# State-space layer with a routed inner layer on one core: matmul order inside a bank, a margin in the planner, and the share of GpSimd

## The chip, the core and the metric

The kernel runs on one core of a Trainium2 chip. The core has five engines that run at the same time, each through its own instructions in order: TensorE (PE, matmul, with the weight load shown apart as PEld), VectorE (DVE), ScalarE (ACT), GpSimd (POOL) and SyncE (SP, which here starts all transfers). They wait for each other on semaphores. The metric is the device time of one execution in microseconds; lower is better. All data is f32.

## What is computed

The input is `u` of 4 sequences, 2048 steps and 256 features. A layer normalization, a selective state-space layer and a residual come first; then a second normalization, a top-2 routed inner layer with low-rank expert parts, and a residual.

```python
def _ssm_forward(u, W_in, b_in, W_x, b_x, W_dt, b_dt, A_log, D, W_out, b_out):
    u_inner = u @ W_in.T + b_in
    x, z = jnp.split(u_inner, 2, axis=-1)
    dbc = x @ W_x.T + b_x
    ...
    delta = jax.nn.softplus(delta_raw @ W_dt.T + b_dt)
    A = -jnp.exp(A_log)
    def step(h, xs):
        dt_t, x_t, Bt, Ct = xs
        dA = jnp.exp(dt_t[..., None] * A)
        dB = dt_t[..., None] * Bt[:, None, :]
        h = h * dA + x_t[..., None] * dB
        y_t = jnp.einsum('bdn,bn->bd', h, Ct)
        return (h, y_t)
    ...
    y = y + x * D
    y = y * (z * jax.nn.sigmoid(z))
    return y @ W_out.T + b_out

def _L0_ffn_ref(x, Wg, bg, Wi, Wo, A, B):
    ...
    base = jnp.einsum('bsd,fd->bsf', x, Wi)
    lora_low = jnp.einsum('bsd,erd->bser', x, A)
    lora = jnp.einsum('bser,efr->bsef', lora_low, B)
    h = jax.nn.relu(base[:, :, None, :] + lora)
    expert_out = jnp.einsum('bsef,df->bsed', h, Wo)
    return jnp.einsum('bse,bsed->bsd', w, expert_out)
```

There are 512 inner channels, 16 states for each, 4 experts of rank 4, and 1024 inner features; `w` holds the weights of the two best experts.

## The kernel before

**Tiles and states.** Time is cut into 16 chunks of 512 steps, four for each sequence. The 512 channels of a chunk are 4 blocks `d` of 128 partitions. For each block and each of the 16 states `n` there is one tile of 128 x 512: with 4 x 16 = 64 of these "states" in a chunk, the main loop (line 924) runs over 1024. Their order is two halves of two blocks each; within a half, groups of four: first block with two `n`, then second block with the same two.

**One state.** `decay` (791): ACT writes exp(a * delta) into one of three PSUM tiles, dA. `enter` (796): POOL multiplies xdt (delta times x) with B, for two states in one operation, into one of three double tiles dBx. `scan` (808): DVE runs the recurrence over dA and dBx, in place in dA. `read` (822): the product of the state with C. DVE writes it as hC, or POOL as hP; POOL does it where `shared` (817) says so, now the first state of each group of four. [...] the scan of a shared state writes to SBUF, as hS. `keep` (831): ACT copies the last column as the carry to the next chunk of the sequence. `sum_y` (836): PE turns the product by four transposing matmuls that add up in the PSUM tile y of its block. `sum_y` runs two loop steps behind the scan, three for a shared state.

**Work beside the loop.** For each chunk, lists of steps run along with the loop. `front` (392) is the normalization of the next chunk, its input projection, delta and softplus, xdt, and the gate with silu; `tail` (524) is the output projection; `ffn` (558) is the second normalization, the routing and the inner layer. Softplus and silu each make ACT load a function table before and after. `layernorm_T` (324) takes statistics on DVE (`stats`), then the reciprocal root on POOL (`rstd`: four small operations), then scales on ACT and transposes on PE.

**The inner layer.** Each chunk has eight rounds `k` (four blocks of 128 steps, two halves of the features). `p_base` starts a PSUM bank with the base product. `p_low` adds to it the low-rank part for the second-best expert, and for the round before the difference that turns this into the best one. `a_relu` takes the ReLU with the expert's weight out of the bank after each. `p_hT` adds both by transposing matmuls into another bank, `a_hT` copies it, and `p_down` makes the down products from two rounds. Three banks of the pool `ps` serve all these and the front's projections; `takes` and `gives` on a step count them.

**Who sets the order.** `Pacer` (45) writes the instructions of each engine in a fixed order at build time. It carries a planned clock for each engine, and each `Step` has a cost. After each scan and each product `fill` (106) lets in those steps whose planned start is close enough to DVE's planned clock; `ready` (126) is the rule. `force` (147) writes a step, with all it needs, at a deadline; `drain` writes what is left after the loop. Nothing of the planning is seen at run time: an engine that meets an operand that is not there waits, and all behind it on that engine.

**The names `xdts`.** Before the loop, `front(0, ...)` returns chunk 0's steps as `xdts` (897). In the loop, line 954 gives the same name the list of the next chunk. Line 952, at state 27, forces `xdts[-1]`.

Of the kernel before, what the change touches and what calls it, by code (L numbers as in the profile page):

```python
# [44 lines left out]
class Pacer:  # L45
# [80 lines left out]
    def ready(self, x):  # L126
        t = self.start(x)
        if t is None:
            return False
        v = self.now["dve"]  # L130
        if self.quiet and x.engine == "act" and x.cost > self.MOST:
            return False
        if x.engine == "dve":
            t = max([y.end for y in x.after if y.engine != "dve"], default=0.0)
            return t + self.LATENCY + self.MARGIN <= v
        return t <= v + self.BEGIN[x.engine] and (t + x.cost <= v + self.END[x.engine] or t <= v - 0.5)

    def drain(self):
# [30 lines left out]
def ssm_moe_layer_kernel(  # L169
# [35 lines left out]
    NN = 2  # L205
    NG = N // NN
    ND2 = 2
    NH = ND // ND2
    CPB = T // TC
    NCHUNK = B * CPB  # L210
    BANKS = 3

    const = ctx.enter_context(tc.tile_pool(name="const", bufs=1))
# [4 lines left out]
    small = ctx.enter_context(tc.tile_pool(name="small", bufs=2))  # L218
# [51 lines left out]
    bm_sb = const.tile([32 * TOPK, F], F32, tag="bm_sb", name="bm_sb")  # L270
# [5 lines left out]
    mhalf = const.tile([P, NJ], F32, tag="mhalf", name="mhalf")  # L276
# [47 lines left out]
    def layernorm_T(src, dst, name, then=None):  # L324

        q = {}

        def stats(j):
            if j == 0:
                q["mv"] = small.tile([P, NJ, 2], F32, tag=f"mv{name[0]}", name=f"mv_{name}")  # L330
            x = small.tile([P, 6], F32, tag="st", name=f"st_{name}_{j}")
            dve.bn_stats(x, src()[:, j, :])
            dve.bn_aggr(q["mv"][:, j, :], x)

        def rstd():

            ve = small.tile([P, NJ], F32, tag="ve", name=f"ve_{name}")
            q["rstd"] = small.tile([P, NJ], F32, tag="rstd", name=f"rstd_{name}")
            q["nmr"] = small.tile([P, NJ], F32, tag="nmr", name=f"nmr_{name}")
            pool.tensor_scalar_add(ve, q["mv"][:, :, 1], EPS)  # L340
            pool.tensor_tensor(q["rstd"], ve, mhalf, ALU.pow)
            pool.tensor_tensor(ve, q["mv"][:, :, 0], q["rstd"], ALU.mult)
            pool.tensor_scalar_mul(q["nmr"], ve, -1.0)

        def norm(j):
            q["xn", j] = work.tile([P, DM], F32, tag=f"xn{j}", name=f"xn_{name}_{j}", bufs=1)
            act.activation(
                q["xn", j], src()[:, j, :], AF.Identity,
                scale=q["rstd"][:, j : j + 1], bias=q["nmr"][:, j : j + 1],
            )  # L350

        def turn(k):
            q["pt", k] = mm_tile(f"pt_{name}_{k}")
            for j in range(NJ):
                pe.transpose(
                    q["pt", k][:, j * P : (j + 1) * P], q["xn", j][:, k * P : (k + 1) * P], ident
                )

        def out_(k):
            if k == 0:  # L360
                q["dst"] = dst()
            act.copy(q["dst"][:, k, :], q["pt", k])

        steps = [Step("dve", 0.54, lambda j=j: stats(j)) for j in range(NJ)]
        steps += [Step("pool", 1.95, rstd)]
        steps += [Step("act", 0.5, lambda j=j: norm(j), locks=j == 0) for j in range(NJ)]
        norms = steps[-1]
        turns = [
            Step("pe", 0.45, lambda k=k: turn(k), after=[norms], takes=1, unlocks=k == KM - 1)
            for k in range(KM)  # L370
        ]
        outs = [Step("act", 0.5, lambda k=k: out_(k), after=[turns[k]], gives=1) for k in range(KM)]
        if then:
            steps.append(then)
        return steps + turns + outs
# [182 lines left out]
    def ffn(c):  # L558

        s = st[c]  # L560
        q = {}
# [96 lines left out]
        HF = F // 2  # L658
        NK = 2 * NJ

        def p_base(k):
            j, half = divmod(k, 2)
            pm = q["z", k] = mm_tile(f"pz_{c}_{k}")
            for m in range(KM):
                pe.matmul(
                    pm, lhsT=s["x2T"][:, m, j * P : (j + 1) * P], rhs=wi_sb[:, m, half * HF : (half + 1) * HF],
                    start=(m == 0), stop=False, skip_group_check=True,
                )

        def p_low(k):  # L670
            for slot, x in ((1, k), (0, k - 1)):
                if 0 <= x < NK:
                    j, half = divmod(x, 2)
                    r = slice(32 * slot, 32 * slot + ER)
                    pe.matmul(
                        q["z", x], lhsT=s["lowT"][r, j * P : (j + 1) * P],
                        rhs=bm_sb[r, half * HF : (half + 1) * HF], start=False, stop=True,
                        skip_group_check=True,
                    )

        def a_relu(k, slot):
            h = q["h", k, slot] = work.tile([P, HF], F32, tag=f"h{slot}", name=f"h{slot}_{c}_{k}")
            act.activation(h, q["z", k], AF.Relu, scale=s["topv"][:, slot, k // 2 : k // 2 + 1])
# [36 lines left out]
        steps = layernorm_T(lambda: s["u"], lambda: new_x2T(c), f"f{c}")  # L720
# [14 lines left out]
        last = steps[-1]  # L735
        for x in steps[-3:]:
            x.after = [steps[steps.index(x) - 1]] + held.get("low", [])
        z1s, hs, copies = [], [], []
        bases = [Step("pe", 1.75, lambda k=k: p_base(k), after=[last], takes=1) for k in range(NK)]
        steps.append(bases[0])  # L740
        for k in range(NK + 1):

            low = Step(
                "pe", 1.06 if 0 < k < NK else 1.05, lambda k=k: p_low(k), after=bases[k : k + 1] + z1s[-1:]
            )
            steps.append(low)
            if k:
                hs.append(Step("act", 0.57, lambda k=k: a_relu(k - 1, 0), after=[low], gives=1))
                steps.append(hs[-1])
            if k < NK:  # L750
                z1s.append(Step("act", 0.57, lambda k=k: a_relu(k, 1), after=[low]))
                steps.append(z1s[-1])
            steps += bases[k + 1 : k + 2]
            if k:
                steps.append(Step("pe", 0.88, lambda k=k: p_hT(k - 1), after=[hs[-1]], takes=1))
                steps.append(Step("act", 0.5, lambda k=k: a_hT(k - 1), after=[steps[-1]], gives=1))
                copies.append(steps[-1])
            for j in range(NJ):
                if k == min(2 * j + 3, NK):
                    for h in range(2):  # L760
                        steps.append(
                            Step("pe", 1.75, lambda j=j, h=h: p_down(j, h), after=[copies[2 * j + 1]], takes=1 - h)
                        )
                    steps.append(Step("dve", 0.33, lambda j=j: add(j), after=[steps[-1]], gives=1))
# [51 lines left out]

    def shared(i):

        c, ib, d, n = states[i]
        return n % NN == 0 and d % ND2 == 0  # L820

    def read(i):
        c, ib, d, n = states[i]
# [70 lines left out]

    spare = small.tile([P, 1], F32, tag="spare", name="spare", bufs=1)
    act.activation(spare, mhalf[:, 0:1], AF.Softplus)
    f, g, dbc, xdts = front(0, front_norm(0))
    pacer.add(f)
    pacer.force(f[2 * NJ])
    join_x()  # L900
# [4 lines left out]
        load_bc(i, 0)  # L905
    for i in range(2):
        load_bc(i, 1)
    pacer.force(xdts[0])

    act.activation(a_sb, a_sb, AF.Exp)  # L910
    dve.tensor_scalar_mul(a_sb, a_sb, -1.0)
    pacer.add(g)
    for i in range(0, AHEAD_B, NN):
        pacer.force(xdts[states[i][2]])
        X[i] = X[i + 1] = pacer.run("pool", 2.32, lambda: enter(i))
    for i in range(AHEAD_A + 1):
        A[i] = pacer.run("act", 0.63, lambda: decay(i))
# [6 lines left out]
    for i in range(M + 4):  # L924
# [24 lines left out]
        if i < M:  # L949
            at = i % PER  # L950
            if i == PER // NH - AHEAD_B - 1:
                pacer.force(xdts[-1])
            if states[i][0] + 1 in deadline:
                dbc, xdts = deadline[states[i][0] + 1]
                if at == PER - 3 * NN * ND2 - 2:
                    pacer.force(dbc)
                if at == PER - AHEAD_B - 6:
                    pacer.force(xdts[0].after[0])
                if at == PER - AHEAD_B - 1:
                    pacer.force(xdts[-1])  # L960
            S[i] = pacer.run("dve", 1.2 if states[i][0] % CPB else 1.14, lambda: scan(i), [A[i], X[i]])
# [72 lines left out]
```

## Time and profile before

| | us |
|---|---|
| median of 3 runs (lowest to highest) | 2129.7 (2126.46 to 2132.01) |
| profiled execution: its own time | 2129.43 |
| its span | 2127.7 |

| group of the page | count | mean ns |
|---|---|---|
| DVE scan into dA, with carry | 576 | 1279 |
| DVE scan into hS, with carry | 192 | 1271 |
| DVE product hC | 768 | 670 |
| POOL product hP | 256 | 1276 |
| POOL product dBx | 512 | 2363 |
| ACT decay dA | 1024 | 693 |
| ACT ReLU h | 256 | 680 |

Each row of the profile names an engine, the output and inputs by the program's names, shapes, count, busy time and mean. Behind the bar stands the idle time of the engine just before these instructions and what ended it. An f32 matmul is two records: the 256 base matmuls stand as x512. Nearly all instructions pass through one helper and so carry its line, L30; they are told apart by their tiles. Idle time that belongs to an engine with time to spare costs nothing.

### The profile page before, as it was taken

How to read it: one execution, taken by the hardware profiler on the slowest of the kernel's cores; microseconds unless marked ns; L12 is line 12 of the kernel's file. 1: busy time of each engine (PE TensorE's matmuls, PEld its weight loads, DVE VectorE, ACT ScalarE, POOL GpSimd, SP SyncE). 2: the span in 40 equal slices, each digit the busy share in tenths (PEclk: the TensorE clock that was granted, in tenths of full speed). 3: DMA queues.
4: the chain of work that ended last, by engine and by line, in shares of the span. 5: the costliest groups of instructions: out<-in, count | busy, mean ns of one | idle time of the engine just before them, and what ended most of it. 6: DMA issues, size and time to landing. Idle time of an engine off the chain costs nothing.

```text
span 2127.7 us, 28591 instructions
## 1 busy us (share of the span) xinstructions
PE 1873.9 (88%) x9504; PEld 1284.0 (60%) x9504; DVE 1855.8 (87%) x2423; ACT 1441.7 (68%) x2898; POOL 1709.4 (80%) x1084
## 2 busy tenths in 40 slices
PE   7768788998889989899899988989899998989978
PEld 4445555665566665657666565766657575666655
DVE  4899898999989989999989998999989999999810
ACT  5857667667676667676767777676677867766522
POOL 5898888989878878888888888888888888878600
PEclk9859799998999999999999999999999999989989
DMA  7454344445444443434435454444535444444200
GB/s 218 144 165 152 127 150 149 149 147 161 151 139 151 149 140 138 169 130 149 163 130 164 140 167 132 147 152 139 169 130 173 136 141 149 138 149 140 98 10 10
DMA packets 106132, 300.70 MB, mean 141 GB/s; under 512 B 12864, under 2 KB 39104, under 8 KB 105984
## 3 DMA queue, kind: packets, MB, share of 16 engines
q1 hardware_dynamic: 105984, 298.88, 42.8%
q8 instruction: 74, 1.21, 0.2%
q14 instruction: 74, 0.61, 0.1%
HBM read 289.41 MB, written 9.44 MB: 140 GB/s over the span
## 4 chain that ended last, share of the span: by engine, by line
PE 25%; DVE 20%; ACT 12%; issue 5%; POOL 1%; DVEq 0%; POOLq 0%; ACTq 0%
DVE dA L30 9%; PE pz L30 9%; PE y L30 5%; PE pf L30 5%; ACT dA L30 5%; DVE hC L30 4%; DVE hS L30 4%; PE phT L30 3%; ACT L30 2%; ACT h L30 1%; PE pin L30 1%; ACT delta L30 1%; ACT g L30 1%; DVE u L30 1%; DVE plg L30 1%
## 5 line engine op out<-in xcount | busy, mean ns | idle before, releaser
L30 POOL TENSOR_TENSOR dBx<-xdt,B 128x1024 f32<-128x1024 f32 x512 | 1207.8, 2363 | 187.5 <-DVE dA L30 157.3
L30 ACT ACTIVATE dA<-delta,a_sb 128x512 f32<-128x512 f32 x1024 | 706.8, 693 | 143.0 <-DVE hC L30 66.8
L30 DVE TENSOR_TENSOR_SCAN dA<-dA,carry,dBx 128x512 f32<-128x512 f32 x576 | 726.4, 1279 | 62.6 <-ACT dA L30 51.0
L30 PE MATMUL y<-ident,hC 128*128 128x128 f32 x3072 | 490.7, 291 | 36.6 <-DVE hC L30 36.5
L30 DVE TENSOR_TENSOR hC<-dA,C 128x512 f32<-128x512 f32 x768 | 514.1, 670 | 0.2 <-issue 0.2
L30 PEld LDWEIGHTS y<-ident,hC 128*128 128x128 f32 x3072 | 386.1, 150 | 181.3 <-issue 73.6
L30 POOL TENSOR_TENSOR hP<-hS,C 128x512 f32<-128x512 f32 x256 | 326.6, 1276 | 5.1 <-issue 4.1
L30 PE MATMUL pz<-wi_sb,x2T 128*128 128x512 f32 x512 | 271.7, 657 | 25.2 <-ACT hT L30 15.4
L30 DVE TENSOR_TENSOR_SCAN dA<-dA,dBx 128x512 f32<-128x512 f32 x192 | 231.2, 1220 | 35.3 <-ACT dA L30 30.5
L30 DVE TENSOR_TENSOR_SCAN hS<-dA,carry,dBx 128x512 f32<-128x512 f32 x192 | 244.1, 1271 | 18.6 <-ACT carry L30 10.6
L30 PE MATMUL pf<-wo_sb,hT 128*128 128x256 f32 x1024 | 243.4, 383 | 11.6 <-ACT hT L30 9.4
L30 PE MATMUL pin<-xnT,w_in_sb 128*128 128x512 f32 x512 | 245.9, 612 | 5.5 <-ACT g L30 3.6
L30 ACT COPY carry<-dA 128x1 f32<-128x1 f32 x576 | 90.1, 157 | 208.5 <-DVE hC L30 206.5
L30 ACT ACTIVATE h<-pz,topv 128x512 f32<-128x512 f32 x256 | 165.4, 680 | 74.1 <-PE pz L30 73.4
L30 PEld LDWEIGHTS pf<-wo_sb,hT 128*128 128x128 f32 x1024 | 186.5, 190 | 41.6 <-ACT hT L30 14.4
L30 PEld LDWEIGHTS y<-ident,hP 128*128 128x128 f32 x1024 | 128.3, 148 | 96.3 <-issue 56.7
L30 PE MATMUL y<-ident,hP 128*128 128x128 f32 x1024 | 167.1, 288 | 18.7 <-POOL hP L30 18.7
L30 PEld LDWEIGHTS pz<-wi_sb,x2T 128*128 128x128 f32 x512 | 95.2, 207 | 124.9 <-issue 76.2
L30 PE MATMUL pz<-bm_sb,lowT 16*128 16x512 f32 x512 | 167.9, 660 | 0.0
L30 PE MATMUL phT<-ident,h 128*128 128x128 f32 x1024 | 139.7, 281 | 21.3 <-ACT h L30 16.8
L30 PEld LDWEIGHTS pin<-xnT,w_in_sb 128*128 128x128 f32 x512 | 92.3, 197 | 93.1 <-issue 75.2
L30 PEld LDWEIGHTS phT<-ident,h 128*128 128x128 f32 x1024 | 120.8, 145 | 44.2 <-ACT h L30 19.5
(94 smaller groups left out, 1784.8 us busy)
## 6 DMA issues: line engine op xcount, KB each, us to landing
B<-bc SPq DMA_DIRECT2D x256, 512.0 KB, 3.7
C<-bc SPq DMA_DIRECT2D x256, 512.0 KB, 3.7
ua<-in_u_dram SPq DMA_DIRECT2D x16, 512.0 KB, 5.5
u<-in_u_dram SPq DMA_DIRECT2D x16, 512.0 KB, 4.4
out_dram<-u SPq DMA_DIRECT2D x16, 512.0 KB, 4.8
w_in_sb<-in_w_inT_dram SPq DMA_DIRECT2D x2, 512.0 KB, 4.7
wi_sb<-in_wiT_dram SPq DMA_DIRECT2D x1, 1024.0 KB, 6.7
wo_sb<-in_woT_dram SPq DMA_DIRECT2D x1, 1024.0 KB, 10.4
```

The costliest lines, as they stand in the source:

```text
L30: return self._tc.keep_in_program_order(f(*args, **kwargs))
```

## The change

Five edits. `shared` gives POOL the products of states 0, 3, 6, 9 and 12 of every 16, five instead of four. `layernorm_T` does the negated mean and the added epsilon on DVE after the last statistics, and two small operations on POOL remain; the planned cost of that step falls from 1.95 to 1.35. In the inner layer the low-rank part of the second-best expert starts the bank, and the base product is added to it; the first ReLU follows the base product. `ready` gets a rule of its own for an ACT step that follows a PE step: it is let in only once PE's planned end lies half a microsecond back. And the first chunk's `xdts` get a name of their own.

```diff
@@ Pacer.ready
+        if x.engine == "act" and any(y.engine == "pe" and y.end + 0.5 > t for y in x.after):
+            t = max(y.end for y in x.after) + 0.5
+            return t <= v + self.BEGIN["act"] and self.now["act"] + 0.5 >= t
         return t <= v + self.BEGIN[x.engine] and (t + x.cost <= v + self.END[x.engine] or t <= v - 0.5)
@@ layernorm_T, stats and rstd
+            if j == NJ - 1:
+                q["nm"], q["ve"] = q["mv"][:, :, 0], q["mv"][:, :, 1]
+                dve.tensor_scalar_mul(q["nm"], q["nm"], -1.0)
+                dve.tensor_scalar(q["ve"], q["ve"], EPS, None, ALU.add)
...
-            pool.tensor_scalar_add(ve, q["mv"][:, :, 1], EPS)
-            pool.tensor_tensor(q["rstd"], ve, mhalf, ALU.pow)
-            pool.tensor_tensor(ve, q["mv"][:, :, 0], q["rstd"], ALU.mult)
-            pool.tensor_scalar_mul(q["nmr"], ve, -1.0)
+            pool.tensor_tensor(q["rstd"], q["ve"], mhalf, ALU.pow)
+            pool.tensor_tensor(q["nmr"], q["nm"], q["rstd"], ALU.mult)
...
-        steps += [Step("pool", 1.95, rstd)]
+        steps += [Step("pool", 1.35, rstd)]
@@ ffn, p_base and p_low
-            pm = q["z", k] = mm_tile(f"pz_{c}_{k}")
+            pm = q["z", k]
...
-                    start=(m == 0), stop=False, skip_group_check=True,
+                    start=False, stop=True, skip_group_check=True,
...
+                    if slot:
+                        q["z", x] = mm_tile(f"pz_{c}_{x}")
...
-                        rhs=bm_sb[r, half * HF : (half + 1) * HF], start=False, stop=True,
+                        rhs=bm_sb[r, half * HF : (half + 1) * HF], start=bool(slot), stop=not slot,
@@ ffn, the rounds
-        bases = [Step("pe", 1.75, lambda k=k: p_base(k), after=[last], takes=1) for k in range(NK)]
-        steps.append(bases[0])
+        bases = []
         for k in range(NK + 1):
             low = Step(
-                "pe", 1.06 if 0 < k < NK else 1.05, lambda k=k: p_low(k), after=bases[k : k + 1] + z1s[-1:]
+                "pe", 1.06 if 0 < k < NK else 1.05, lambda k=k: p_low(k), after=[last] + z1s[-1:], takes=int(k < NK)
             )
             steps.append(low)
             if k:
                 hs.append(Step("act", 0.57, lambda k=k: a_relu(k - 1, 0), after=[low], gives=1))
                 steps.append(hs[-1])
             if k < NK:
-                z1s.append(Step("act", 0.57, lambda k=k: a_relu(k, 1), after=[low]))
-                steps.append(z1s[-1])
-            steps += bases[k + 1 : k + 2]
+                bases.append(Step("pe", 1.75, lambda k=k: p_base(k), after=[low]))
+                z1s.append(Step("act", 0.57, lambda k=k: a_relu(k, 1), after=bases[-1:]))
+                steps += [bases[-1], z1s[-1]]
@@ shared
-        c, ib, d, n = states[i]
-        return n % NN == 0 and d % ND2 == 0
+        return i % 16 in SHARED
@@ before and in the loop
+    SHARED = (0, 3, 6, 9, 12)
...
-    f, g, dbc, xdts = front(0, front_norm(0))
+    f, g, dbc, first_xdts = front(0, front_norm(0))
...
-                pacer.force(xdts[-1])
+                pacer.force(first_xdts[-1])
```

More of the change, by code (lines that the diff above doesn't have):

```diff
@@ L333, in stats @@
             dve.bn_aggr(q["mv"][:, j, :], x)
+            if j == NJ - 1:
+                q["nm"], q["ve"] = q["mv"][:, :, 0], q["mv"][:, :, 1]
+                dve.tensor_scalar_mul(q["nm"], q["nm"], -1.0)
+                dve.tensor_scalar(q["ve"], q["ve"], EPS, None, ALU.add)
         def rstd():
-            ve = small.tile([P, NJ], F32, tag="ve", name=f"ve_{name}")
             q["rstd"] = small.tile([P, NJ], F32, tag="rstd", name=f"rstd_{name}")
             q["nmr"] = small.tile([P, NJ], F32, tag="nmr", name=f"nmr_{name}")
-            pool.tensor_scalar_add(ve, q["mv"][:, :, 1], EPS)
-            pool.tensor_tensor(q["rstd"], ve, mhalf, ALU.pow)
-            pool.tensor_tensor(ve, q["mv"][:, :, 0], q["rstd"], ALU.mult)
-            pool.tensor_scalar_mul(q["nmr"], ve, -1.0)
+            pool.tensor_tensor(q["rstd"], q["ve"], mhalf, ALU.pow)
+            pool.tensor_tensor(q["nmr"], q["nm"], q["rstd"], ALU.mult)
         def norm(j):
@@ L907, in ssm_moe_layer_kernel @@
         load_bc(i, 1)
-    pacer.force(xdts[0])
+    pacer.force(first_xdts[0])
     act.activation(a_sb, a_sb, AF.Exp)
@@ L913, in ssm_moe_layer_kernel @@
     for i in range(0, AHEAD_B, NN):
-        pacer.force(xdts[states[i][2]])
+        pacer.force(first_xdts[states[i][2]])
         X[i] = X[i + 1] = pacer.run("pool", 2.32, lambda: enter(i))
```

## The prediction

> **What bounds the kernel now.** I read the busy table and the slices first, then the busy time by stretch, the waits, and the timelines of one silu and of the tail.
>
> ```profile
> PE 1873.9 (88%) x9504; PEld 1284.0 (60%) x9504; DVE 1855.8 (87%) x2423; ACT 1441.7 (68%) x2898; POOL 1709.4 (80%) x1084
> ...
> DVE  4899898999989989999989998999989999999810
> ...
> POOL 5898888989878878888888888888888888878600
> ...
> L30 POOL TENSOR_TENSOR dBx<-xdt,B 128x1024 f32<-128x1024 f32 x512 | 1207.8, 2363 | 187.5 <-DVE dA L30 157.3
> ```
>
> The averages do not choose between DVE, PE and POOL. The slices show the shape: DVE is full until about 2010 us, and then two slices are almost without it. So the span is three pieces. The first scan starts at 31.6 us (timeline). The last sum over states ends on PE at 2018.4, so the loop of 1024 states takes 1986.8, or 1.94 a state. The tail, with the inner layer of the last two chunks on PE, takes 2127.7 - 2018.4 = 109.3.
>
> Busy time by half chunk (32 states each; columns: length, then busy PE, PEld, DVE, ACT, POOL, granted clock, DMA share, GB/s):
>
> ```profile
> 1455.96:1512.07 56.11, 54.31 (x310) 39.94 (x309) 54.97 (x63) 34.80 (x57) 48.19 (x26) 1.00 0.47 151
> 1512.07:1578.08 66.01, 56.82 (x267) 38.08 (x266) 59.71 (x90) 51.60 (x102) 56.37 (x41) 0.87 0.48 152
> ```
>
> The quick half has DVE at 98%, POOL at 86%. The slow half, with softmax, normalizations, softplus and silu, leaves DVE 6.3 us idle. DVE paces the loop; POOL mostly waits for DVE to free a buffer (157.3 us). What holds DVE is ACT:
>
> ```profile
> DVE dA L30 <- ACT dA L30: 81.5, 129, 6.1
> ...
> ACT dA L30 <- DVE hS L30: 65.4, 78, 1.6
> ACT hT L30 <- PE phT L30: 61.9, 62, 3.9
> ACT h L30 <- PE pz L30: 40.7, 53, 3.7
> ```
>
> (The waits between 31.6 and 2018.4: total, times, longest.) DVE also waits 21.0 us for ACT's carry copies before scans into hS. Meanwhile ACT, in order, stands 61.9 + 40.7 us at PE results of the inner layer. The decay it owes DVE stands behind them.
>
> **Products moved to GpSimd.** 256 of 1024 go to POOL now, 320 after: 64 fewer on DVE. Records on DVE overlap, so I take the spacing of starts:
>
> ```profile
> 1273.89 0.67 DVE L30 TENSOR_TENSOR g<-g,py 128x512 f32<-128x512 f32 x1
> 1274.48 0.67 DVE L30 TENSOR_TENSOR hC<-dA,C 128x512 f32<-128x512 f32 x1
> 1275.07 1.27 DVE L30 TENSOR_TENSOR_SCAN hS<-dA,carry,dBx 128x512 f32<-128x512 f32 x1
> 1276.26 0.66 DVE L30 TENSOR_TENSOR hC<-dA,C 128x512 f32<-128x512 f32 x1
> 1279.01 1.29 DVE L30 TENSOR_TENSOR_SCAN dA<-dA,carry,dBx 128x512 f32<-128x512 f32 x1 [2.09 <-ACT dA L30]
> ```
>
> A product costs 1275.07 - 1274.48 = 0.59 us: 64 x 0.59 = **-38** of pure DVE time. The scan costs the same either way (1279 ns into dA, 1271 into hS).
>
> Against that, a state without a product on DVE makes the next scan come 0.59 sooner, and then ACT's decay is late. After the hS scan at 1351.21 the scan at 1353.24 starts 0.84 after the product before it, not 0.59, its idle marked as a wait for ACT's dA: 0.25. I find it at about half to two thirds of such places between 1263 and 1334. With 0.2 for each of 64 new places: **+13** (0 if the new places have their decay in time; +38 if every one gives all back).
>
> The skill speaks against the move: GPSIMD Engine Reference, Engine selection, gives elementwise products with two inputs to VectorE, GpSimd being about twice as slow. The rows agree on the ratio (hP 1276 ns, hC 671), and by the rule alone 64 x 1.276 = 82 us come in for 38 out, +44. But those 82 count only on the path, and the 157.3 us that POOL waits for DVE can hold them. So I take the trace's sum and keep the rule's as the ground of the slower rival. The cover is thin in the quick half: 48.2 of 56.1 busy, two more products (+2.6), and the order of instructions puts the four xdt of the next chunk (4 x 1.27 = 5.1) at about state 36 of 64, from the slow into the quick half. That makes 55.9 of some 55.5: at par. POOL may start a dBx four scans and their products before it is needed, some 7 us, of which its own 2.36 is part; so POOL can run some 4.5 late, and a burst of 5.1 hardly shows. PE then waits longer for hP (18.7 us over 15 waits now), which DVE does not feel, since no hC waits for PE now. I charge nothing to the forecast.
>
> **LayerNorm.** Of four small POOL operations per normalization two go (228 and 242 ns, x32: POOL -15 us, off the path). DVE gains two on 128x4. Nearest rows: a dependent operation of that size follows the next in 0.21 (reciprocal 1285.72, product 1285.93), an independent one in 0.10 (1290.67 to 1290.77). The first waits for the statistics, so 0.2: 64 x 0.2 = **+13** (6 to 14). DVE is the pacing engine, so it is paid in full.
>
> **Low-rank part first, and the margin.** The matmuls are the same and equally long (660 ns for the low-rank, 657 for the base), so PE's work does not change. A bank is taken one base product later, and the two ReLUs come apart: now they run as a pair (1.27 us on ACT, between two decays), afterwards one has the base product and the other the transposes as cover. The margin lets an inner-layer ACT step into the order only 0.5 us after PE's planned end. DVE's waits for ACT are 81.5 + 7.8 + 21.0 plus small ones, about 111. At the start lie 12. The 32 table-loading blocks for silu and softplus (2.09 lost at the one above, 1.58 and 0.74 at others; 1.4 on average) keep about 45, as silu is forced at the same states. The places after hS hold about 27. The last 27 are what ACT's standing at PE can cause, and I take half: **-14** (0, nothing, to -45, all of it and most of the places). What is queued behind an ACT step that waits is the next decay, and behind it the scan.
>
> **First delta.** The forced step at state 27 meant the first chunk's last xdt, but the name had been rebound to the next chunk's; all of that chunk's front was forced early. It cost DVE 6.07 us, its longest wait for dA (scan at 89.99). After, softplus 1 comes at state 55, at a block like any other (about 2): **-4**, once (0 to -6).
>
> **Tail.** By the order of instructions, after the last sum 15 of chunk 14's 32 inner bank matmuls, 40 of 64 transposes and 24 of 32 down products are left now; afterwards all of them, so 17, 24 and 8 more. In the dense tail a round takes 3.84 (bank products 2.9, transposes 0.94) and a set of 8 down products 3.6: 17 x 0.72 + 24 x 0.12 + 8 x 0.45 = 19 us more. But now PE has a hole there: the output projection's matmuls end at 2053.6, the routing of chunk 15 keeps PE nearly empty until 2072.9, and the first base product then takes double:
>
> ```profile
> 2071.89 1.06 PE L30 MATMUL plT<-ident,lowm 128*64 128x128 f32 x4 [6.05 <-POOL lowm L30]
> 2072.75 3.62 PE L30 MATMUL pz<-wi_sb,x2T 128*128 128x512 f32 x4
> ...
> 2077.59 1.98 PE L30 MATMUL pz<-wi_sb,x2T 128*128 128x512 f32 x4
> ```
>
> After, the projection stands before chunk 14's rounds, and the routing lies inside them. From the last sum: 2.5 (copy, transposes, gate), 7.2 projection, 4.2 other route matmuls, two inner layers of 8 x 3.84 + 4 x 3.6 = 45.1 each, 1.5 at the end of the second, 1.5 of round waits, and 4.3 from the last matmul to the end: 111. So **+2** (-3 if the waits of 0.68 before each pair of down products go, +19 if nothing hides).
>
> **Sum.** -38 + 13 + 13 - 14 - 4 + 2 = -28, against the span of 2127.7: 2100. The profiled execution took 2129.43, 1.7 more than its span, and the median of 2129.7 lies 0.3 above that. So **2102**.
>
> **Rivals.**
> - *ACT was the real brake* (0.18): the margin removes most of what DVE waits for outside the table loads, 45 instead of 14, and new places cost nothing. 2102 - 31 - 13 = 2058; with half of the second, 2066. For it: 102 us of standing at PE. Against: half lies where DVE is not waiting.
> - *Hidden anyway* (0.15): the places after hS give back all 38, or the later steps of the inner layer keep all of chunk 14's 19 us in the tail. +25 or +17 on the forecast: 2127 or 2119, say 2123. For it: one place in two waits already, and the order does leave a whole layer behind.
> - *GpSimd becomes the bound, slower* (0.17): in the quick halves, if each of the 16 dBx keeps its wait of about 0.5 for its scan (0.53 and 0.58 in the timeline near 1350) although POOL has 55.9 to do. A half then takes up to 55.9 + 8 = 64, where the forecast has 56. If a third of these waits stays, 58.6: 16 x 2.6 = 42 on the forecast, 2144. It decides once POOL's work and waits together pass DVE's some 55.5. Against: an engine that is behind finds its scan already done.
> - That the change does not do what it says is shut out: the order has 320 products on POOL and 704 on DVE.
>
> **How the numbers follow.** Forecast 0.50 at 2102, its own range 2082 to 2118 from the unknown costs. With the rivals, 2064 to 2140 leaves out the far ends of the first and the last, under 2 in 10. A change of 0.3% is 6.4 us, about what this measurement can tell from none. Faster: all of the forecast, the ACT case, and half of the hidden one, 0.75; the same 0.07; slower 0.18.
>
> **What would show it.** hC x704 and hP x320, and DVE's busy time down by some 30. POOL's busy about +67, its wait for DVE's dA below 157.3 and few DVE waits for POOL (else the third rival). ACT's waits for PE phT and pz well below 61.9 + 40.7, and DVE's for ACT dA near 70. No 6 us wait near state 27. The last sum near 1987, and a tail of about 111 without the hole after the projection. A loop no shorter than 1986 would make the prediction wrong, as would a tail of 125.

## The result and the profile after

| | before, us | after, us |
|---|---|---|
| median of 4 runs (lowest to highest) | 2130.64 (2126.46 to 2132.01) | 2097.06 (2088.33 to 2101.31) |
| span of the profiled execution | 2127.7 | 2086.4 |
| first scan to last sum, 1024 states | 1986.8 | 1943.3 |
| the same, DVE busy / DVE idle | 1841.2 / 145.6 | 1834.6 / 108.7 |
| from the last sum to the end | 109.3 | 111.2 |

The ratio is 0.9841 [0.9825, 0.9857]: 33.6 us less. The profiled execution of after is the quickest of its four, 8.7 below their median, so a difference of spans shows some 9 us more than one of medians. The predicted 2102 lies 5 us above the result.

These are the busy table, two rows of the slices, and three of the costliest groups, all from the page of after:

```profile
PE 1844.4 (88%) x9504; PEld 1275.2 (61%) x9504; DVE 1851.3 (89%) x2423; ACT 1429.9 (69%) x2898; POOL 1764.6 (85%) x1084
...
DVE  4989999998989999999999999999999999999810
POOL 5999999898989989898888998889899898989700
...
L30 POOL TENSOR_TENSOR dBx<-xdt,B 128x1024 f32<-128x1024 f32 x512 | 1206.2, 2361 | 106.4 <-DVE dA L30 40.7
...
L30 DVE TENSOR_TENSOR hC<-dA,C 128x512 f32<-128x512 f32 x704 | 471.8, 670 | 0.0
L30 POOL TENSOR_TENSOR hP<-hS,C 128x512 f32<-128x512 f32 x320 | 407.5, 1273 | 7.9 <-DVE hS L30 3.9
```

The 64 products have moved (704 and 320), POOL is 55 us busier, and it waits 40.7 us for DVE's dA where it waited 157.3. DVE, which lost 64 products, is only 4.5 us less busy over the whole span. That is the first thing that does not fit.

The waits between the first scan and the last sum of after (total, times, longest):

```profile
DVE dA L30 <- ACT dA L30: 58.9, 79, 3.0
...
ACT dA L30 <- DVE hS L30: 48.1, 65, 3.0
...
ACT h L30 <- PE pz L30: 25.4, 39, 3.4
...
ACT hT L30 <- PE phT L30: 9.0, 19, 1.0
```

ACT now stands 34.4 us at the inner layer's results, where it stood 102.6, and DVE waits 58.9 us for its decay, not 81.5. So the table says where the 43.5 us of the loop come from: 36.9 are idle time of DVE, and only 6.6 are its work. Not all of that idle time is the margin's doing, as u_ln shows below.

The work has gone into two groups that the prediction put at 13 us. They stand in the groups of after, kept apart by shape (busy, mean ns):

```profile
L30 DVE TENSOR_SCALAR mv_a<-mv_a 128x4 f32<-128x4 f32 x32 | 26.2, 863 | 0.6
...
L30 DVE TENSOR_SCALAR mv_f<-mv_f 128x4 f32<-128x4 f32 x32 | 12.1, 424 | 0.6
```

Together 38.3 us, as much as the 64 products were worth. On mv_a an operation on 128 x 4 takes 863 ns on average, longer than a product on 128 x 512 (670). The answer for the tile mv_a (lowest, median, highest ns; first and last start) puts it beside a neighbour of the same size on the same tile:

```profile
L30 DVE BATCH_NORM_AGGREGATE mv_a<-st_a x64: 181/182/184, 5.1 to 1689.3; 128x2 f32<-128x6 f32 x64
L30 DVE TENSOR_SCALAR mv_a<-mv_a x32: 155/544/2398, 7.0 to 1689.7; 128x4 f32<-128x4 f32 x32
```

The aggregate is always alike; the new operations take anything from 155 to 2398 ns. Two stretches of the timelines of DVE and POOL in after show what decides (start, length in us; x2 joins two operations):

```profile
1069.28 2.69 DVE L30 TENSOR_SCALAR mv_a<-mv_a 128x4 f32<-128x4 f32 x2
1069.59 2.35 POOL L30 TENSOR_TENSOR dBx<-xdt,B 128x1024 f32<-128x1024 f32 x1
...
171.09 0.24 DVE L30 TENSOR_SCALAR mv_f<-mv_f 128x4 f32<-128x4 f32 x2
171.41 1.01 POOL L30 TENSOR_TENSOR rstd_f<-mv_f,mhalf 128x4 f32<-128x4 f32 x1 [1.23 <-DVE mv_f L30]
```

In the first, the pair on DVE ends at 1069.28 + 2.69 = 1071.97, and POOL's dBx at 1071.94. In the second POOL stands idle, waiting for this very pair, and the pair takes 0.24. All records of after say the same. Of its 64 small operations 26 last more than 260 ns, and each of these ends 23 to 30 ns after an operation of POOL; in none of the other 38 does an operation of POOL run from before its start until after its end. So the reading to be tested is that these small operations are *held* on DVE until POOL's operation has ended. The longest, 2636 ns on mv_f, outlasts the end of a product on POOL and the whole dBx that follows it. The Trainium skill has a rule for it, which the prediction did not weigh: SBUF — State Buffer, Who interferes with whom. By it VectorE has a second pair of ports that it shares with GpSimd under an exclusive lock; `tensor_scalar` may enter a mode that takes that pair, and the loser blocks fully; an operation with two SBUF inputs contends with GpSimd's reads, while one with at most one SBUF input, outside those modes, does not. The product hC, which reads dA from PSUM and C from SBUF, agrees: each of its 704 records lies between 656 and 686 ns, with POOL 85% busy. So does the routing's comparison, a `tensor_scalar` that reads the PSUM tile plg:

```profile
L30 DVE TENSOR_SCALAR m<-plg 128x16 f32<-128x16 f32 x32 | 4.1, 169 | 0.6
```

Its 32 records lie between 164 and 174 ns, though 12 of them fall wholly within an operation of POOL.

### The profile page after: what moved, and what is told of

The parts are those of the page before. It is cut to its first block, busy times and chain, and to the rows that moved or that the text cites. A ratio compares the mean times of both kernels' runs of the same rounds, so it can differ in the third digit from the quotient of the medians.

```text
span 2086.4 us, 28685 instructions
## 1 busy us (share of the span) xinstructions
PE 1844.4 (88%) x9504; PEld 1275.2 (61%) x9504; DVE 1851.3 (89%) x2423; ACT 1429.9 (69%) x2898; POOL 1764.6 (85%) x1084
## 5 line engine op out<-in xcount | busy, mean ns | idle before, releaser
L30 POOL TENSOR_TENSOR dBx<-xdt,B 128x1024 f32<-128x1024 f32 x512 | 1206.2, 2361 | 106.4 <-DVE dA L30 40.7
L30 DVE TENSOR_TENSOR_SCAN dA<-dA,carry,dBx 128x512 f32<-128x512 f32 x528 | 662.4, 1278 | 49.1 <-ACT dA L30 41.4
L30 PE MATMUL y<-ident,hC 128*128 128x128 f32 x2816 | 442.7, 290 | 34.8 <-DVE hC L30 34.6
L30 DVE TENSOR_TENSOR hC<-dA,C 128x512 f32<-128x512 f32 x704 | 471.8, 670 | 0.0
L30 PEld LDWEIGHTS y<-ident,hC 128*128 128x128 f32 x2816 | 352.5, 150 | 120.0 <-DVE hC L30 52.3
L30 POOL TENSOR_TENSOR hP<-hS,C 128x512 f32<-128x512 f32 x320 | 407.5, 1273 | 7.9 <-DVE hS L30 3.9
L30 DVE TENSOR_TENSOR_SCAN hS<-dA,carry,dBx 128x512 f32<-128x512 f32 x240 | 305.2, 1272 | 15.6 <-ACT dA L30 8.3
L30 PE MATMUL pz<-wi_sb,x2T 128*128 128x512 f32 x512 | 257.6, 627 | 0.0
L30 PEld LDWEIGHTS y<-ident,hP 128*128 128x128 f32 x1280 | 162.7, 149 | 147.4 <-issue 79.7
L30 PE MATMUL y<-ident,hP 128*128 128x128 f32 x1280 | 209.8, 289 | 39.8 <-POOL hP L30 39.7
L30 DVE TENSOR_TENSOR_SCAN dA<-dA,dBx 128x512 f32<-128x512 f32 x176 | 211.1, 1219 | 26.1 <-ACT dA L30 17.5
L30 PEld LDWEIGHTS pin<-xnT,w_in_sb 128*128 128x128 f32 x512 | 91.9, 196 | 90.4 <-issue 75.0
```

The costliest lines, as they stand in the source:

```text
L30: return self._tc.keep_in_program_order(f(*args, **kwargs))
```

## Experiments on LayerNorm

**u_ln: after, with the four small operations on POOL again.** The theory: the held operations cost the changed kernel their length. The rival: DVE has slack for them.

```diff
-                dve.tensor_scalar_mul(q["nm"], q["nm"], -1.0)
-                dve.tensor_scalar(q["ve"], q["ve"], EPS, None, ALU.add)
...
+            pool.tensor_scalar_add(ve, q["mv"][:, :, 1], EPS)
             pool.tensor_tensor(q["rstd"], ve, mhalf, ALU.pow)
...
+            pool.tensor_scalar_mul(q["nmr"], ve, -1.0)
```

> The changed kernel with the two small LayerNorm operations back on GpSimd, as before (four operations there, none added on VectorE); the other four edits kept. Port theory: in the changed kernel's trace the 64 VectorE operations on 128x4 show 38.3 us of records instead of the 13 predicted, and the long ones end within 0.1 us of a GpSimd operation, so they are held while GpSimd has the shared port. Then taking them away gives VectorE some 36 us back, part of it lost again to waits for ScalarE: 2065 to 2082, ratio to before 0.970 to 0.978, and no stretched small operation on VectorE. Rival, cover: these stalls lie where VectorE would wait for a decay anyway, and GpSimd gets 15 us more to do: no gain, 2092 to 2102, ratio 0.982 to 0.987.

Measured: 2072.18 us (2069.74 to 2072.95), ratio to before 0.9728 [0.9712, 0.9744]. This is 25 us quicker than after, and the quickest of all kernels here. The busy table of its page:

```profile
PE 1839.2 (89%) x9504; PEld 1268.8 (61%) x9504; DVE 1815.6 (88%) x2359; ACT 1430.3 (69%) x2898; POOL 1779.1 (86%) x1148
```

POOL does 64 operations and 14.5 us more, and the kernel is still quicker; DVE has 35.7 less. In the loop alone DVE's busy time falls by 35.3 against after and its idle time grows by 18.6 (127.3 against 108.7), which leaves 16.7. So about half of what the operations hold DVE is given back: while it stands, ACT's decays get ahead. DVE's wait for ACT's dA, 58.9 in after, is 70.6 here. The cost is 17 us by the two profiled loops and 25 by the medians (24 when each is set against before on its own chip). That DVE was held is shown by its records. How much of the net cost is the hold is not: the edit also puts the planned cost of the step on POOL back to 1.95, and in the two traces the order of instructions on PE, ACT and DVE differs from the first chunks on. A kernel with the order of after and unheld operations was not run.

**o_ln: before, with this edit alone.** The kernel before, where POOL is 80% busy and not 85%, gets the lines that u_ln loses.

```diff
+                dve.tensor_scalar_mul(q["nm"], q["nm"], -1.0)
+                dve.tensor_scalar(q["ve"], q["ve"], EPS, None, ALU.add)
...
-            pool.tensor_scalar_add(ve, q["mv"][:, :, 1], EPS)
...
-            pool.tensor_scalar_mul(q["nmr"], ve, -1.0)
```

> The kernel before with the LayerNorm edit alone; TensorE's order of instructions is that of before. Port theory: 64 small operations on VectorE are held by GpSimd, 20 to 38 us of records instead of 13 (GpSimd is less busy here, 80% instead of 85%, so nearer the lower end), and GpSimd's 15 us less buys nothing: 2142 to 2160, ratio 1.006 to 1.014. Rival, by the prediction's price of 0.2 us each and cover by waits: 2126 to 2142, ratio 0.998 to 1.006.

The order on PE did not stay that of before: the traces differ from the first chunk on, where the transposes of the normalization stand at other places. The planned cost of the step, 1.35 instead of 1.95, is part of this edit.

Measured: 2136.82, ratio 1.0029 [1.0017, 1.0041]. It is slower, but by 6 us, inside the range of the rival and below that of the theory. The records are shorter here, 17.6 + 6.7 = 24.3 us, with means of 593 and 253 ns. DVE's busy time in the loop grew by 22.9, its idle time fell by 21.3 (145.6 to 124.3). So it is held here too, and in the loop, 1.5 us longer in all, gets nearly all of it back: DVE has more waits here to get it back from. The tail of this profiled execution is 5.5 longer (114.8), and that is not LayerNorm's: PE has the same 378 matmuls there and is busy 95.7 us with them, where it was busy 90.4 before, at a granted clock of 0.86 and not 0.91. So of the 6 us by the medians LayerNorm may have as little as 1.5. The price of a held operation is not a constant: it is what DVE does not have to wait for anyway.

**lnTT: after, with two-input operations in place of the tensor_scalar pair.** The narrow theory: only `tensor_scalar` takes the shared pair, so another operation is not held. The wide one: any operation of DVE with a second SBUF input is.

```diff
-                dve.tensor_scalar_mul(q["nm"], q["nm"], -1.0)
-                dve.tensor_scalar(q["ve"], q["ve"], EPS, None, ALU.add)
+                dve.tensor_tensor(q["nm"], q["nm"], mone, ALU.mult)
+                dve.tensor_tensor(q["ve"], q["ve"], meps, ALU.add)
...
```

> The changed kernel with the two small VectorE operations of each LayerNorm as tensor_tensor against constant tiles of -1 and epsilon, so with two inputs in SBUF[...]. If only the two-port mode is held (port theory in its narrow form), the 64 operations take 0.16 to 0.25 us each, 10 to 16 us in all: 2074 to 2086. If any second read through the shared port is held while GpSimd reads[...], records stay stretched, 25 us or more in all, and the time stays at the changed kernel's: 2088 to 2102.

Measured: 2096.47, ratio 0.984 [0.9823, 0.9858], the time of after, with the same order of instructions on PE, ACT and DVE. Two of its groups:

```profile
L30 DVE TENSOR_TENSOR mv_a<-mv_a,meps 128x4 f32<-128x4 f32 x16 | 18.1, 1132 | 0.0
...
L30 DVE TENSOR_TENSOR mv_a<-mv_a,mone 128x4 f32<-128x4 f32 x16 | 11.0, 685 | 0.6
```

With the pair on mv_f (10.9 and 2.5) this makes 42.5 us. The wide theory holds: both forms are held, and again each record over 260 ns ends with an operation of POOL, 17 to 24 ns after it. That the page's mode of `tensor_scalar` is what held the first form is not shown, as a trace does not name the mode. In its favour: in after, the reciprocal on 128 x 4, also in place in SBUF with one input, takes 177 or 178 ns in all 16 records, 8 of them wholly within an operation of POOL.

## Experiments on the products and the first delta

**u_shared: after, with four products of 16 on POOL.**

```diff
-    SHARED = (0, 3, 6, 9, 12)
+    SHARED = (0, 4, 8, 12)
```

> The changed kernel with four of 16 products on GpSimd, as before; the other four edits kept. By the prediction's sum (38 us less on VectorE, 13 given back after hS scans) it is 25 us slower than the changed kernel: 2117 to 2127. Rival, given back: GpSimd's load and the earlier scans eat it all: within 5 us of the changed kernel, 2092 to 2102.

Measured: 2119.46, ratio 0.9947 [0.9929, 0.9965], 22 us above after. DVE's busy time in the loop is 1861.6, 27 more than in after, and its small operations are held for 25.2 us, not 38.3: a less busy POOL holds them less, which hides 13 of the 38. The two profiled executions lie 31 apart, 24 in the loop and 8 in the tail (119.2), where PE again waits 6.04 us for the routing of the last chunk. In the loop the products are worth those 24 here and 34 without the LayerNorm edit (o_first to o_sharedfirst, below). That the longer held operations are the reason for this difference is likely, but not shown.

**o_shared: before, with five of 16 alone.**

```diff
-        c, ib, d, n = states[i]
-        return n % NN == 0 and d % ND2 == 0
+        return i % 16 in SHARED
```

> The kernel before with only the five of 16 products. By the prediction's sum -38 + 13 = -25, as taking it out of the changed kernel cost 22: 2103 to 2111. Rival: without the margin the earlier scans wait more for ScalarE and half is lost: 2112 to 2122, VectorE's waits for dA above 95 us.

Measured: 2106.52, ratio 0.9886 [0.9865, 0.9907], 24.8 less. The number fits and hides something. From the timeline of its DVE, near state 27:

```profile
83.73 0.67 DVE L30 TENSOR_TENSOR hC<-dA,C 128x512 f32<-128x512 f32 x1
108.66 1.23 DVE L30 TENSOR_TENSOR_SCAN dA<-dA,dBx 128x512 f32<-128x512 f32 x1 [24.26 <-ACT dA L30]
```

DVE stands still for 24 us, once. It is the forced front of the next chunk, which cost 6.07 us at this place before. The other edits of after meet the same place, so the name `first_xdts` has to be looked at together with the products.

**u_first, o_first and o_sharedfirst: the name.** u_first is after with the old name; o_first is before with only the new one; o_sharedfirst is before with five products and the new name.

u_first:

```diff
-                pacer.force(first_xdts[-1])
+                pacer.force(xdts[-1])
...
```

> The changed kernel with the old name for the first chunk's xdt, so that the next chunk's front is forced at state 27; the other four edits kept. TensorE's order differs in the first chunks only. Prediction: 4 us slower than the changed kernel, a wait of VectorE of about 6 us for a decay near 90 us, 2096 to 2106. Rival: the forced work is only moved, and the first 64 states end at the same time: 2092 to 2100.

Measured: 2116.64, ratio 0.9932 [0.9907, 0.9956], 20 above after.

o_first:

```diff
-                pacer.force(xdts[-1])
+                pacer.force(first_xdts[-1])
...
```

> The kernel before with only the first chunk's xdt under a name of its own. In the changed kernel the old name cost a wait of 23 us, because with the margin nearly nothing of the next front had been let in by state 27. Theory: here much of that front is in by then (its first projection stands at state 15), the wait at state 27 was 6.07 us, so the edit alone brings 4 to 8 us: 2122 to 2127, and no wait of over 4 us near 90 us. Rival: the name is worth 20 us by itself: 2107 to 2114.

Measured: 2122.83, ratio 0.9963 [0.9948, 0.9977], 8.5 less than before (5 to 11 by the interval). In the profiled execution the first 64 states are 2.2 shorter and the loop 8.0. The rest comes in later chunks, where all engines have the order of before, so that it is no work that the name moved; its cause is not shown.

o_sharedfirst:

```diff
-        return n % NN == 0 and d % ND2 == 0
+        return i % 16 in SHARED
...
-                pacer.force(xdts[-1])
+                pacer.force(first_xdts[-1])
...
```

> The kernel before with the five of 16 products and the first chunk's own name, without margin, new bank order and LayerNorm edit. With the five products alone VectorE stood 24.3 us at the forced front of state 27, so the products, not the margin, keep the next front from being in by then. Theory: that stall goes to about 2 us and nothing else changes (the order of TensorE is the same from chunk 2 on): 2081 to 2091, and the first 64 states take 108 to 114 us instead of 136.9. The products would then be worth over 38 us. Rival: the stall hid other waits, and the front's work costs the time later: 2095 to 2106.

Measured: 2088.14 (2087.23 to 2089.07), ratio 0.9797 [0.978, 0.9813], 43 less than before. Two edits of five do better than all five. DVE's busy time in the loop is 1802.7, 38.5 less than before, and its idle time 142.3, against 145.6. Set against o_first, from which it differs by the products alone, it is 35 quicker: DVE's busy time falls by 39.2 (1841.9 there) and its idle time grows by 5.3 (136.9 there).

What makes the stall 24 us and not 6? The time from the first scan over 64 states tells the two suspects apart, the products and the margin:

| with the old name, but for the last row | first 64 states, us |
|---|---|
| four products (before) | 118.7 |
| four products, bank order and margin (o_lowmargin, below) | 118.9 |
| five products (o_shared) | 136.9 |
| five products and all other edits (u_first) | 134.2 |
| new name, five products (o_sharedfirst) | 111.8 |

It is the products; that the margin alone does it, as one of the expectations had it, is shut out. (From o_shared to o_sharedfirst the first 64 states become 25 us shorter but the whole loop only 14, though the order behind the first chunks is the same on all engines. So two profiled loops of one order can differ by some 10 us, and a difference of loops is no better than that.)

From the timeline of ACT in u_first, while DVE stands:

```profile
82.52 2.07 ACT L30 ACTIVATE xn_a<-ua,nmr_a,rstd_a 128x256 f32<-128x256 f32 x4 [3.96 <-POOL nmr_a L30]
...
90.73 0.69 ACT L30 ACTIVATE xT<-pin,b_in_sb 128x512 f32<-128x512 f32 x1 [1.23 <-PE pin L30]
...
96.94 2.59 ACT L30 ACTIVATE delta<-pdt,b_dt_sb 128x512 f32<-128x512 f32 x4 [0.36 <-PE pdt L30]
99.54 1.28 ACT L30 ACT_TABLE_LOAD   x1
```

The whole front of chunk 1 runs in one piece, from scaling by POOL's root on, and the next decay stands behind it at 104.11. When POOL starts that root, 14 scans have started in before (13 in u_shared), 29 in o_shared and u_first, and 34 with five products and the new name: with more products on POOL the planner lets the root in later. So at state 27 nothing of this front behind the statistics is done, and the deadline with the wrong name forces all of it. Before, most of it had been done: behind the decay at 80.82, the last one ahead of the wait, ACT had three of the four deltas and the softplus left.

**ln6: u_ln with six of 16.** If DVE still paces the loop, 64 more products off it should gain again.

```diff
-    SHARED = (0, 3, 6, 9, 12)
+    SHARED = (0, 3, 6, 8, 11, 14)
```

> LayerNorm on GpSimd as in u_ln, and six of 16 products on GpSimd instead of five. For 16 states GpSimd then has 8 x 2.363 + 6 x 1.276 = 26.6 us, VectorE 16 x 1.19 + 10 x 0.59 = 24.9: the prediction's third rival, GpSimd as the bound. If it holds, the loop gets no shorter than u_ln's 1926 in spite of 38 us less on VectorE, VectorE waits for GpSimd (over 30 us), and by the order the tail grows by some 30 as part of chunk 13's inner layer is left: 2095 to 2135. Rival, GpSimd still has room through its waits: loop 15 us or more shorter than u_ln, and 2080 to 2095 with the tail.

Measured: 2153.33, ratio 1.012 [1.0099, 1.0142]; the loop takes 1967.2 where that of u_ln takes 1926.6, the tail 148.5. This is worse than expected. POOL is busy 1841.8 of the loop's 1967.2, 94%. Waits of ln6 over the whole span:

```profile
PE y L30 <- POOL hP L30: 114.6, 72, 5.4
...
DVE hS L30 <- ACT carry L30: 62.9, 19, 10.2
...
DVE hS L30 <- POOL dBx L30: 13.2, 11, 3.2
```

DVE waits for POOL directly only some 33 us in all, and for ACT 165. Part of that goes back to POOL by way of PE, which, in order, stands at y for POOL's product (39.7 us in the loop of after); that ACT's results stand behind these waits fits the rows, but no run separates it. Another part is again the planner's: 19 of the 41 us that the loop is longer than that of u_ln lie in the first 64 states. There POOL's root of the next normalization comes late once more, ACT stands 5.33 us for it at 121.14, and DVE's next scan starts only at 129.06, after its longest wait for a carry, 10.20. So POOL is near its limit here, the place of the third rival; at five products that was not reached (DVE waits for POOL in after: 7.6, 3.5 and less). Of the 78 us between the two profiled executions the tail has another 37, with more of the inner layer left (594 matmuls after the last sum, 452 in u_ln).

## Experiments on the inner layer's banks and the margin

**o_lowmargin: before, with the new order in the bank and the margin.**

```diff
+        if x.engine == "act" and any(y.engine == "pe" and y.end + 0.5 > t for y in x.after):
+            t = max(y.end for y in x.after) + 0.5
+            return t <= v + self.BEGIN["act"] and self.now["act"] + 0.5 >= t
...
-                    start=(m == 0), stop=False, skip_group_check=True,
+                    start=False, stop=True, skip_group_check=True,
...
```

> The kernel before with the new order inside the bank and the margin, without the other three edits. Theory of the prediction: these two together take 14 us of VectorE's waits for ScalarE, and the tail grows by 5 to 10 as more of chunk 14 is left: 2118 to 2130. If they are worth what taking each out of the changed kernel cost (12 and 26), 2092 to 2112.

Measured: 2112.41, ratio 0.9907 [0.9879, 0.9936], 18.9 less than before. From o_sharedfirst to u_ln, which adds the same two edits, it is 16 by the medians, and 14 when each is set against before on its own chip. In the loop DVE waits some 14 us less for ACT, but not at dA (84.8, before 81.5): what fell are its waits before scans into hS, for ACT's carry (21.0 to 11.9) and for the decay (7.8 to nearly nothing).

**u_margin: after without the three lines of the margin.**

> The changed kernel without the margin for ScalarE in the planner; the other four edits kept. Theory: the margin keeps decays from standing behind ScalarE steps that wait for TensorE, worth the 34 us by which VectorE's waits for ScalarE fell; then without it 2115 to 2130, and ScalarE's waits for phT and pz near the 60 and 40 us of before. Rival: the new order inside the bank, not the margin, took these waits away (the two ReLUs come apart): 2090 to 2102, and the waits stay low.

Measured: 2109.24, ratio 0.9909 [0.9891, 0.9928], 12 above after. Waits in its loop:

```profile
ACT h L30 <- PE pz L30: 84.3, 84, 4.3
...
DVE dA L30 <- ACT dA L30: 65.6, 109, 2.9
```

Without the margin ACT stands three times as long at the bank (25.4 in after) with the same matmuls, while its wait for the transposes, phT, stays short (8.3 in the loop, 61.9 before). So the new order of the bank alone only moves ACT's waits, 102.6 us before and 92.6 here, from phT to pz; the margin makes them short. The time lies between the ranges of the theory and of the rival.

**u_low: after with the old order in the bank.** The rounds are those of before, the margin stays.

```diff
-                    start=False, stop=True, skip_group_check=True,
+                    start=(m == 0), stop=False, skip_group_check=True,
...
```

> The changed kernel with the old order inside the bank (base product first, then the low-rank part); the other four edits kept. By the order of instructions the inner layer then falls further behind: after the last sum all of chunk 14's rounds and a part of chunk 13's are left. Theory: the new bank order is what lets the margin be paid for; without it the tail grows by 20 us or more and the loop keeps its gain: 2112 to 2130. Rival: the bank order matters by itself in the loop, through the paired ReLUs: loop 15 us longer and tail longer, over 2135.

Measured: 2123.18, ratio 0.9963 [0.9951, 0.9975], 26 above after. In the profiled execution, 4 above its median, the loop is even 3.5 shorter than that of after (1939.8), and the tail is 154.3 against 111.2: PE has 558 matmuls left after the last sum, where it has 452 in after. With the old order the margin keeps so much of the inner layer back that PE has it to do alone at the end. Taking out either edit costs 12 or 26 us, together more than the 14 to 19 that both bring, so no share of the gain belongs to one of them.

## Why the prediction was right, and where it was not

The sum was -28 and the result -33.6, but not by the same terms. LayerNorm cost 11 us more than it was priced, the give-back cost 8 less, and the first delta brought 5 more. That these errors nearly cancel is luck.

| step | predicted | measured |
|---|---|---|
| 64 products off DVE | -38 | -38.5 of DVE's busy time in the loop (o_sharedfirst) |
| given back after scans into hS | +13 | +5 of DVE's idle time (o_sharedfirst against o_first) |
| LayerNorm on DVE | +13 | +24 in the changed kernel (17 by the loops), +6 or less alone |
| bank order and margin | -14 | -19 alone, -14 beside products and name |
| first delta | -4 | -8.5 alone, -20 in the changed kernel |
| tail | +2 | +1.9 (111.2, predicted 111) |

Added one after the other, products and name make -43, bank and margin -14 and LayerNorm +24: -34. The four parts put alone into before make -8.5 - 24.8 - 18.9 + 6.0 = -46, which misses by nearly 13: the parts do not add up, LayerNorm least of all. (Each difference is against the median of before on the same chip, 2129.6 to 2131.5, but for the -20, which is u_first against after.)

**Products: right.** The spacing of starts, 0.59, was the right price, not the record's 0.67.

**The give-back: over-sized.** "With 0.2 for each of 64 new places" took the late decay after each scan into hS for a cost of the move. Against o_first the move made DVE's idle time 5.3 longer, not 13 (the medians agree: 35 us quicker for 39 of DVE's busy time), and not at these places: before a scan that follows one into hS, DVE stood idle 34.6 us in all (256 places) in o_first and 26.7 (320 places) in o_sharedfirst. What was lost was lost before other scans (84.1 and 92.3) and before other operations (16.9 and 20.9). Why the 64 new places cost nothing was not shown.

**LayerNorm: the price of one operation was mis-sized.** 0.2 us was taken from dependent operations of that size elsewhere on DVE (reciprocal to product), which were not held in those places. The records mean 0.86 and 0.42. The step also said that, on the pacing engine, it "is paid in full"; about half is by the profiled loops, some two thirds by the medians. The section that the prediction weighed, on engine selection, says nothing of this.

**First delta: mis-sized.** The prediction priced the wait that it could see, 6.07, as a thing of its own. With five products the wait at the same forced step is 24, so what the new name saves belongs to the products as well.

**Bank order and margin: right,** -14 beside the products. The prediction named ACT's standing at PE, and that is what went: 102.6 to 34.4. It expected the gain in DVE's wait for dA; put alone into before, the two edits brought it in the waits before scans into hS.

**The tail: right.** The timeline of PE in after, from the last output projection of the loop on:

```profile
1976.36 3.62 PE L30 MATMUL po<-w_out_sb,g 128*128 128x256 f32 x16
1981.36 0.63 PE L30 MATMUL plT<-ident,lowm 128*64 128x128 f32 x4 [1.38 <-POOL lowm L30]
...
2023.87 1.86 PE L30 MATMUL plg<-wga_sb,x2T 128*128 128x20 f32 x16
2025.58 3.70 PE L30 MATMUL pf<-wo_sb,hT 128*128 128x256 f32 x16
...
2031.77 0.63 PE L30 MATMUL plT<-ident,lowm 128*64 128x128 f32 x4
```

The routing of the last chunk (plg to plT) lies among the rounds of chunk 14, and the wait of 6 us before plT is gone. A whole layer more after the last sum costs 2 us, as it fills that hole. The granted clock of the tail also rose, from 0.91 to 0.99: 452 matmuls keep PE busy for 104.1 us, where 378 took 90.4.

Of what was to be seen in the profile: the counts came out exactly. DVE's busy time fell by 4.5 instead of 30, as the held operations took the difference. POOL's rose by 55 instead of 67. DVE's waits for ACT dA came to 58.9 (predicted near 70, which is what u_ln has without the held operations), the last sum at 1975.2 (predicted near 1987). ACT was not the real brake: the margin and the bank order brought 14 to 19 us, not the 45 of that rival. In its second half it was nearer, as the new places cost nothing. (Its sum, 2102 - 31 and half of 13, gives 2064 or 2065, not 2066.) The gain was not hidden, and GpSimd was not yet the bound.

Still open: how much of LayerNorm's cost is the changed order of instructions, how much of u_shared's 22 us is more than tail and hold, and why the decays after hS did not cost more.

## What to carry to other kernels

A small operation moved to a free-looking place can be priced by what runs beside it, not by its size: look at the spread of its records, and if the long ones end with another engine's operations, they are held. A sum of single edits is only as good as the places that they share; here a deadline that cost 6 us cost 24 once the plan on another engine had shifted. And when one engine is relieved by giving work to a second, look for the second one's lateness at the engines between them.

## What the hardware showed unexpectedly

Operations of DVE on 128 x 4 in SBUF, 155 ns when POOL stands still, took up to 2636 ns in after beside operations of POOL, and every one over 260 ns ended 23 to 30 ns after one of these. It happened to `tensor_scalar` with one SBUF input and a constant (means 863 and 424 ns) and to `tensor_tensor` with two SBUF inputs (means 1132, 685 and 684 ns; the fourth group, at 154, was not held). It did not happen to other operations with one SBUF input: the aggregate statistics on the same tile (181 to 184 ns, 58 of 64 wholly within an operation of POOL) and the reciprocal (177 or 178). Nor did it to a `tensor_scalar` that reads PSUM (164 to 174 ns), nor to the product of a PSUM and an SBUF tile (656 to 686 ns). A mean hides this kind of delay; the lowest, the median and the highest of a group show it at once.

The tail of o_ln shows another thing that is easily taken for a cost of the edit: the same 378 matmuls kept PE busy 5.3 us longer at a granted clock of 0.86 than at 0.91.
